# Half-logarithms of layer 2's row work on VectorE, a queue of its own for group 0, and a new placing of checks and waits in a four-layer graph kernel

## The chip, the cores and the metric

The kernel runs on one core of a Trainium2 chip. The core has a tensor engine for matrix products (TensorE; PE in the profile), a vector engine (VectorE, DVE), a scalar engine that evaluates functions from tables (ScalarE, ACT), a general engine (GpSimd, POOL), and a sequencer that issues most transfers here (SyncE, SP). [...] The metric is the device time of one execution in microseconds (us), given as the median of several executions.

## The reference

The input is a feature matrix x of 4096 rows by 64 features and an adjacency matrix adj of 4096 by 4096 zeros and ones. Four layers follow each other, each adding its result to its input and normalising every row:

```python
x = _layernorm(x + _L0_gnn_ref(x, adj, W, b))              # mean of neighbours, linear map, relu
x = _layernorm(x + _L1_gnn_ref(x, adj, r, w_att, b_att))   # hyperbolic attention
x = _layernorm(x + _L2_gnn_ref(x, adj, weight, bias))      # weights 0.5 ** (rank of the neighbour)
x = _layernorm(x + _L3_gnn_ref(x, adj, att_w, att_b))      # hyperbolic attention
```

Layers 1 and 3 weigh every edge with a sigmoid of a left number of the row and a right number of the neighbour. Both numbers come from `logmap0(x)`, whose factor is artanh(n)/n of the row's norm n; artanh is half the logarithm of (1+n)/(1-n). Layer 2 needs, for each row, the rank of each neighbour counted from the end, so that its weight is 2 to the power of minus that rank.

## The kernel before

The 4096 rows are cut into 4 groups of 1024 columns of the transposed adjacency matrix (`GROUPS` is 3, 2, 1, 0, in that order) and 32 blocks of 128 (also taken from the last to the first). Every layer reads the whole matrix again: `load(s, g)` (line 696) brings two blocks of one group, 1 MB, into one of 6 buffers called `edges`, through SyncE's queue; g runs from 15 down to 0. A buffer is used again six loads later, once its matmuls and its check are done.

`check` (line 834) is a test on VectorE that a loaded tile holds only zeros and ones; each tile is checked once in the whole kernel. Half of the checks are made in layer 0 (even g, line 1405) and half in layer 2 (odd g, `load_2`, line 1576).

Layer 0 and both attention layers run their passes one group at a time. Layer 2 runs a wide pass over groups 3 and 2 together (`wide_pass`, line 1517), then a narrow pass over group 1 and one over group 0 (`narrow_pass`, line 1544). Per block and half, TensorE counts neighbours into a `z` tile (`count`, line 1583), ScalarE takes an exponential of it (`weights_of`, line 1592), and TensorE multiplies the result with `halves`, the features times the layer's weight matrix.

What is done per row between the layers (here called row work) is written as Python generators. `later` puts a generator into one of two queues; `tick` takes each queue's first generator a step further, and a step says with `yield n` after how many ticks the next one may come. So ticks decide at which block of a pass the instructions of row work are written down. `need(tag)` ticks until the tagged work is written, however many ticks that takes, before the pass goes on. The order of TensorE and ScalarE is the written order (`FIXED`, line 589); the other engines are ordered by a planner from its own cost estimates. In the wide pass the first five blocks have no tick; from block 26 on there are two per block.

The generators that matter here:

- `move` (line 1096) turns an attention layer's sums for one group into new rows. For groups 3, 2 and 1 its row numbers are computed on GpSimd (with some steps on VectorE), for group 0 on VectorE. `pool_done` (line 661) gives the ticks that it leaves GpSimd. It ends with the rows of the next layer.
- `supports` (line 1245) follows the `move` of layer 1: a 16-bit copy of the rows on ScalarE and its remainder on GpSimd, 8 transposes, a copy on ScalarE, 16 small matmuls, a copy on ScalarE and a subtraction on VectorE give `halves` for the group. The wide pass needs group 1 before block 15 (tag `(2, 1)`) and group 0 before block 7 (tag `(2, 0)`).
- `attention` (line 1456) queues these: `supports` of groups 3, 2 and 1 in the second queue, `move` of each group in the first, and for the last group, group 0, both in the first queue, behind the `move` of group 1.
- `end_2` (line 1486), `norm_rows` (line 860) and `prepare` (line 880) turn the sums of layer 2 into the rows, factors and transposed features of layer 3. `prepare` also serves layer 1. Its second part, among casts and transposes, computes `t` (the norm) and `q1` (its square) on VectorE and takes two logarithms on ScalarE (lines 948 and 949); VectorE combines them (line 968) and forms left and right. In layer 3, groups 3 and 2 are prepared within the narrow passes, group 1 within the second one, group 0 at the start of the attention.

Between the exponentials of layer 2 and these logarithms ScalarE loads a table of functions, and another one to go back.

## Time and profile before

| what | value |
|---|---|
| runs | 1088.86, 1088.87, 1093.16 us; median 1088.87 |
| the profiled execution's own time | 1089.49 us |
| its span, first to last instruction | 1087.7 us |
| busy: TensorE, VectorE, ScalarE, GpSimd | 996.7, 913.4, 761.7, 265.0 us |
| layer 0, about 0 to 200 us | DMA busy 95% |
| attention of layer 1, about 200 to 511 us | TensorE busy 305.3 of 311 us |
| layer 2's wide pass, 511 to 617 us | TensorE busy 98.0 of 106 us |
| layer 2's narrow passes, 617 to 736 us | TensorE busy 104.9, ScalarE 98.1 of 119 us |
| attention of layer 3, 736 to 1050 us | TensorE busy 306.9 of 314 us |
| the end, 1050 to 1087.7 us | VectorE busy 22.5 of 37.7 us |

The span lies within the execution's own time; 1.8 us are around it. A line of the profile's timeline gives the start and the duration in us, the engine, the line of the kernel, the operation, the tiles written and read with their shapes, and in square brackets how long the engine had been idle before it and what ended that wait. A line with "x2" merges two instructions in a row. Layer 2 is the stage whose lines are named L1587 (counting), L1594 (exponential), L1599 and L1553 (sums). An `ACT_TABLE_LOAD` is ScalarE's change of its function table.

### The profile page before, as it was taken

The numbers are of one execution on the slowest core, as the hardware profiler recorded it, in microseconds if no ns is written. First come the engines' busy times: TensorE is split into PE (matmuls) and PEld (weight loads), VectorE is DVE, ScalarE is ACT, GpSimd is POOL, SyncE is SP. The second block draws the span as 40 slices with busy tenths as digits, with TensorE's granted clock in tenths as the row PEclk, the third lists the DMA queues.
The fourth block names the chain that finished last, engine by engine and source line by source line (L and its number), as shares of the span: only waits on it lengthen the run. The fifth ranks groups of instructions, "written<-read, shape, count | busy, mean of one in ns | idle before, by whom it ended". The sixth has DMA issues, their size and how long they took to land.

```text
span 1087.7 us, 13618 instructions
## 1 busy us (share of the span) xinstructions
PE 996.7 (92%) x4845; PEld 404.7 (37%) x4845; DVE 913.4 (84%) x1451; ACT 761.7 (70%) x888; POOL 265.0 (24%) x649
## 2 busy tenths in 40 slices
PE   5998998899999999999998988899899999999970
PEld 2455554233333333333333333443333333333320
DVE  6677978999999999999456494738999999999976
ACT  0003123879888989887675778889798988888850
POOL 0011211010154433514600010100001544344162
PEclk9998999899999999999999999999999999999995
DMA  9999999636576566655887988887366766666400
GB/s 344 399 418 378 359 427 390 223 130 242 194 252 213 199 230 214 230 200 185 309 302 295 359 289 291 283 280 256 131 224 210 254 210 218 240 217 226 148 1 23
DMA packets 38580, 271.62 MB, mean 250 GB/s; under 512 B 4710, under 2 KB 4710, under 8 KB 5734
## 3 DMA queue, kind: packets, MB, share of 16 engines
q1 hardware_dynamic: 37728, 270.03, 68.1%
q8 instruction: 40, 0.66, 0.2%
q10 hardware_dynamic: 774, 0.63, 0.2%
q14 instruction: 38, 0.31, 0.1%
HBM read 269.58 MB, written 1.05 MB: 249 GB/s over the span
## 4 chain that ended last, share of the span: by engine, by line
PE 62%; DVE 24%; ACT 6%; POOL 2%; DMA 2%; issue 2%; ACTq 0%; SPq 0%; POOLq 0%; DVEq 0%
PE acc L1035 17%; PE z L1587 9%; PE z L1057 8%; PE z L1063 7%; PE z L1060 7%; DVE t L1080 6%; DVE t L1078 6%; PE acc L1412 4%; DVE junk L836 3%; ACT sq L1594 2%; DMA edges<-in_adj_dram 2%; PE acc L1599 2%; ACT sq L1075 1%; PE z L1599 1%; PE aux L941 1%
## 5 line engine op out<-in xcount | busy, mean ns | idle before, releaser
L1078 DVE SCALAR_TENSOR_TENSOR t<-z,sig 128x1024 f32<-128x1024 f32 x256 | 309.9, 1220 | 13.9 <-ACT sq L1075 11.8
L1080 DVE SCALAR_TENSOR_TENSOR t<-sq,t 128x2048 f32<-128x2048 f32 x128 | 295.3, 2307 | 0.2
L1075 ACT ACTIVATE sq<-z 128x1024 f32<-128x1024 f32 x256 | 254.7, 1021 | 57.8 <-PE z L1063 25.6
L1072 ACT ACTIVATE sig<-left_b,right 128x1024 f32<-128x1024 f32 x256 | 287.2, 1149 | 3.9 <-DVE t L1078 2.9
L1035 PE MATMUL acc<-t,xe 128*64 128x512 f32 x1024 | 258.1, 610 | 10.9 <-DVE t L1080 10.7
L1057 PE MATMUL z<-edges,two_i 128*128 128x512 bf16 x512 | 202.5, 395 | 6.3 <-DVE t L1078 6.3
L1063 PE MATMUL z<-dst,src 74*128 74x512 f16 x512 | 196.4, 384 | 0.0
L1060 PE MATMUL z<-lo_hi,hi_lo 128*128 128x512 f16 x512 | 195.3, 381 | 0.0
L1594 ACT ACTIVATE sq<-z 128x512 bf16<-128x512 f32 (+1 forms) x192 | 136.7, 740 | 51.2 <-PE z L1587 48.0
L1035 PEld LDWEIGHTS acc<-t,xe 128*64 128x64 f32 x1024 | 64.0, 137 | 139.4 <-issue 105.9
L836 DVE SCALAR_TENSOR_TENSOR t<-edges 128x2048 bf16<-128x2048 f32 x32 | 73.0, 2287 | 35.2 <-DMA edges<-in_adj_dram 34.9
L1587 PE MATMUL z<-edges,pass_by 128*128 128x512 bf16 x248 | 89.1, 400 | 11.3 <-ACT sq L1594 10.9
L1412 PE MATMUL acc<-edges,first 128*128 128x512 bf16 x256 | 82.9, 406 | 14.3 <-DMA edges<-in_adj_dram 14.2
L1057 PEld LDWEIGHTS <-two_i 128*128 128x128 bf16 x512 | 50.4, 98 | 120.5 <-issue 74.5
L1587 PE MATMUL z<-edges,enter 128*128 128x512 bf16 x256 | 91.2, 399 | 0.0
L1412 PE MATMUL acc<-edges,third 128*65 128x512 bf16 x256 | 82.3, 404 | 0.0
L1063 PEld LDWEIGHTS <-src 74*128 74x128 f16 x512 | 49.5, 97 | 73.3 <-issue 11.8
L836 DVE SCALAR_TENSOR_TENSOR junk<-edges 128x2048 bf16<-128x2048 f32 x32 | 73.1, 2285 | 4.3 <-DMA edges<-in_adj_dram 4.0
L1060 PEld LDWEIGHTS <-hi_lo 128*128 128x128 f16 x512 | 50.4, 99 | 62.9 <-issue 17.4
L867 POOL TENSOR_TENSOR sq<-z 128x512 f32<-128x512 f32 x8 | 14.2, 1778 | 157.1 <-DVE z L866 134.0
L1131 POOL TENSOR_TENSOR w_att<-x,u 128x512 f32<-128x512 f32 x6 | 12.7, 2123 | 147.8 <-ACT u L1126 147.8
L1412 PEld LDWEIGHTS <-third 128*65 128x65 bf16 x256 | 29.3, 114 | 34.4 <-issue 5.4
(381 smaller groups left out, 981.5 us busy)
## 6 DMA issues: line engine op xcount, KB each, us to landing
edges<-in_adj_dram SPq DMA_DIRECT2D x256, 1024.0 KB, 4.9
x<-in_x_dram SPq DMA_DIRECT2D x4, 256.0 KB
out_dram<-x ACTq DMA_DIRECT2D x2, 256.0 KB
out_dram<-x SPq DMA_DIRECT2D x2, 256.0 KB
w_sb<-in_L_gnn_W_dram ACTq DMA_DIRECT2D x1, 32.0 KB, 4.8
w_twice<-in_L_gnn_weight_dram ACTq DMA_DIRECT2D x2, 16.0 KB, 7.8
given<-in_L_gnn_b_dram ACTq DMA_DIRECT2D x1, 0.2 KB
given<-in_L_gnn_bias_dram ACTq DMA_DIRECT2D x1, 0.2 KB
```

The source lines that it names most:

```text
L836: V.scalar_tensor_tensor(junk, a, 0.0, a, ALU.not_equal, ALU.not_equal, accum_out=odd[:, n : n + 1])
L1035: it = nc.tensor.matmul(acc[h * D : (h + 1) * D, :], xe[:, j, :], t[:, k, h * W : (h + 1) * W], start=j == BLOCKS[0], stop=j == BLOCKS[-1],)
L1057: nc.tensor.matmul(half, two_i, edge[:, at : at + W], start=True, stop=False)
L1060: nc.tensor.matmul(half, hi_lo[:, of], lo_hi[:, to], start=False, stop=False)
L1063: last = nc.tensor.matmul(half, src[:, of], dst[:, to], start=False, stop=True)
L1072: nc.scalar.activation(sig, left_b, AF.Sigmoid, bias=right[:, j : j + 1])
L1075: nc.scalar.activation(sq[:, k], zp, AF.Square, bias=ROOT + OFF, scale=-1.0 / UNIT)
L1078: V.scalar_tensor_tensor(t[:, k], zp, 0.0, sig, ALU.max, ALU.mult)
L1080: V.scalar_tensor_tensor(t, sq, HIGH**2, t, ALU.add, ALU.mult)
L1412: nc.tensor.matmul(accs[h][:m], lhs[:, j, :], edge[:, at : at + W], start=j == BLOCKS[0], stop=j == BLOCKS[-1],)
L1587: nc.tensor.matmul(z[:, h : h + W], lhs, rhs[:, h : h + W], start=j == BLOCKS[0], stop=True, skip_group_check=True,)
L1594: weighed[0] = nc.scalar.activation(w, z[:, :n], AF.Exp, bias=-(OFF_EDGE + CUT) * LN2, scale=-LN2)
```

## The change

It has five parts. `half_log_of_ratio` computes half the logarithm of (1+t)/(1-t) from (1+t) squared over (1-q): exponent and mantissa are taken apart by bit operations, and the mantissa's logarithm is a polynomial; all on VectorE. `prepare` calls it in layer 3 for groups 3, 2 and 1 in place of the two logarithms; group 0 and layer 1 keep them. A third queue takes `move` and `supports` of group 0 at the end of layer 1's attention. `checked_later` leaves the checks of g = 15 and 13 of groups 3 and 2 to layer 0 and those of g = 2 and 0 to layer 2. `pool_done` counts fewer ticks while layer 2 runs. So that the `move` of group 0 can run beside that of group 1, its `u` goes into another buffer, `z0`, and its sums are copied by VectorE.

```diff
--- before.py
+++ after.py
@@ -49,6 +49,8 @@
 MEAN_TOP = 1e-10
 
 LN2 = 0.6931471805599453
+ROOT2 = 2.0**0.5
+LOG = (0.3333341, 0.1998662, 0.14984541)
 OFF_EDGE = 255.0
 CUT = 27.0
 SUP = 512.0
@@ -588,7 +590,7 @@
 
             FIXED = {mybir.EngineType.PE, mybir.EngineType.Activation}
             ROW_ENGINES = FIXED | {mybir.EngineType.DVE}
-            queues, place, done, held = ([], []), [0, 0], set(), []
+            queues, place, done, held = ([], [], []), [0, 0], set(), []
 
 
 
@@ -627,7 +629,7 @@
                     mark(True)
 
             def later(steps, second=False, wait=0):
-                queues[second].append([steps, place[1] + wait])
+                queues[int(second)].append([steps, place[1] + wait])
 
             def in_turn(tag, *parts):
                 for part in parts:
@@ -640,7 +642,7 @@
 
             def need(tag):
                 while tag not in done:
-                    assert queues[0] or queues[1], tag
+                    assert any(queues), tag
                     tick(1)
 
             def soon():
@@ -660,6 +662,8 @@
 
             def pool_done(small, large=0):
 
+                if place[0] == 2:
+                    return 2 + int((small * 0.29 + large) / 1.45)
                 return 2 + int(small * 0.33 + large)
 
             spare, turn_of = [], [0]
@@ -698,6 +702,10 @@
                 nc.sync.dma_start(a, adj[s, :, 2 * g : 2 * g + 2, :])
 
                 return a, a.rearrange("p b i -> p (b i)").bitcast(BF16)[:, 1::2]
+
+            def checked_later(s, g):
+
+                return g in (0, 1, 2, 3, 5, 7, 9, 11) if s in GROUPS[:2] else g % 2 == 1
 
             def grp(name, bufs=None):
                 kw = {"bufs": bufs} if bufs else {}
@@ -856,6 +864,32 @@
                 V.tensor_scalar(sc, root, -((2.0 * UNIT) ** 0.5), None, ALU.mult)
                 V.tensor_scalar(short, root, least, None, ALU.mult)
                 return c, c2, sc, rsc, of_y, root, short, by_root, by_short
+
+            def half_log_of_ratio(t, q):
+
+                a, e, d = nums("log_a"), nums("log_e"), nums("log_d")
+                V.tensor_scalar(q, q, -1.0, 1.0, ALU.mult, ALU.add)
+                V.reciprocal(q, q)
+                V.tensor_scalar(a, t, 1.0, None, ALU.add)
+                V.tensor_mul(a, a, a)
+                V.tensor_mul(a, a, q)
+                V.tensor_scalar(
+                    e.bitcast(I32), a.bitcast(I32), 0x7F800000, None, ALU.bitwise_and
+                )
+                V.tensor_scalar(
+                    a.bitcast(I32), a.bitcast(I32), 0x007FFFFF, 0x3F800000,
+                    ALU.bitwise_and, ALU.bitwise_or,
+                )
+                V.tensor_scalar(e, e.bitcast(I32), 2.0**-23, -126.5, ALU.mult, ALU.add)
+                V.tensor_scalar(d, a, ROOT2, None, ALU.add)
+                V.reciprocal(d, d)
+                V.scalar_tensor_tensor(a, a, -ROOT2, d, ALU.add, ALU.mult)
+                V.tensor_mul(d, a, a)
+                V.tensor_scalar(q, d, LOG[2], None, ALU.mult)
+                V.scalar_tensor_tensor(q, q, LOG[1], d, ALU.add, ALU.mult)
+                V.scalar_tensor_tensor(q, q, LOG[0], d, ALU.add, ALU.mult)
+                V.scalar_tensor_tensor(q, q, 1.0, a, ALU.add, ALU.mult)
+                V.scalar_tensor_tensor(t, e, 0.5 * LN2, q, ALU.mult, ALU.add)
 
             def norm_rows(layer, s, v, x2_to):
 
@@ -927,6 +961,9 @@
                     V.tensor_mul(t, q1, rt)
                     V.tensor_scalar(t, t, TOP, None, ALU.min)
                     V.tensor_scalar(q1, q1, QTOP, None, ALU.min)
+                    by_log = layer == 3 and s != GROUPS[-1]
+                    if by_log:
+                        half_log_of_ratio(t, q1)
                     yield 2 * near()
                     for into, rows_of in (
                         (hi_lo, ys[:, :, : 2 * D]),
@@ -945,8 +982,9 @@
                         nc.scalar.copy(into[:, cols], turned[:n])
                         held.pop()
                         yield 1
-                    nc.scalar.activation(t, t, AF.Ln, bias=1.0)
-                    nc.scalar.activation(q1, q1, AF.Ln, bias=1.0, scale=-1.0)
+                    if not by_log:
+                        nc.scalar.activation(t, t, AF.Ln, bias=1.0)
+                        nc.scalar.activation(q1, q1, AF.Ln, bias=1.0, scale=-1.0)
                     yield from free()
                     p = take(F32, P, WB, 7)
                     for k in range(WB):
@@ -965,8 +1003,11 @@
                     )
                     V.tensor_mul(own, m, p[:, :, 6])
                     held.pop()
-                    V.scalar_tensor_tensor(f, q1, -0.5, t, ALU.mult, ALU.add)
-                    V.tensor_mul(f, f, rt)
+                    if by_log:
+                        V.tensor_mul(f, t, rt)
+                    else:
+                        V.scalar_tensor_tensor(f, q1, -0.5, t, ALU.mult, ALU.add)
+                        V.tensor_mul(f, f, rt)
                     V.scalar_tensor_tensor(f, f, SERIES0, q, ALU.add, ALU.add)
                     V.tensor_mul(f, f, m)
                     yield 1
@@ -1114,8 +1155,11 @@
                     all_u = ys.rearrange("p k f -> p (k f)").bitcast(F32)[:, : WB * (D + 1)]
                     all_u = all_u.rearrange("p (k f) -> p k f", f=D + 1)
                 else:
-                    all_u = row.tile([P, WB, D + 1], F32, name="u_1")
-                u, sum_1 = all_u[:, :, :D], all_u[:, :, D]
+                    all_u = None if last else row.tile([P, WB, D + 1], F32, name="u_1")
+                if all_u is None:
+                    u, sum_1 = grp("z0"), nums("sum_1")
+                else:
+                    u, sum_1 = all_u[:, :, :D], all_u[:, :, D]
                 for part in range(2):
                     yield from free()
                     t = take(F32, P, 2, 2, D + 1)
@@ -1123,9 +1167,18 @@
                         cols = slice((2 * part + i) * P, (2 * part + i + 1) * P)
                         nc.tensor.matmul(t[:, i], sums[:, cols], centre, start=True, stop=True)
                     yield near()
-                    nc.scalar.copy(
-                        all_u.rearrange("p (h k) f -> p k h f", h=2)[:, 2 * part : 2 * part + 2], t
-                    )
+                    of = slice(2 * part, 2 * part + 2)
+                    if all_u is None:
+                        nc.scalar.copy(
+                            u.rearrange("p (h k) f -> p k h f", h=2)[:, of], t[:, :, :, :D]
+                        )
+                        V.tensor_copy(
+                            sum_1.rearrange("p (h k) -> p k h", h=2)[:, of], t[:, :, :, D]
+                        )
+                    else:
+                        nc.scalar.copy(
+                            all_u.rearrange("p (h k) f -> p k h f", h=2)[:, of], t
+                        )
                     held.pop()
                     yield near()
                 E.tensor_mul(w, xg, u)
@@ -1402,7 +1455,7 @@
                             a, edge = load(s, g)
                             if s == GROUPS[0] and 2 * g % WB == WB - 2 and g > WB // 2:
                                 parts_of(2 * g // WB - 1)
-                            if g % 2 == 0:
+                            if not checked_later(s, g):
                                 check(s, g, a, own.tile([P, 2, WW], BF16, name="junk"))
                             for k in (1, 0):
                                 j = 2 * g + k
@@ -1468,9 +1521,10 @@
                             in_turn((layer + 1, s + 1), there((layer, s + 1, "moved")), behind(s + 1)),
                             True, 9,
                         )
-                    later(move_s)
+                    apart = 2 if n + 1 == NW and layer == 1 else 0
+                    later(move_s, apart)
                     if n + 1 == NW:
-                        later(in_turn((layer + 1, s), behind(s)))
+                        later(in_turn((layer + 1, s), behind(s)), apart)
                 anchored[0] = False
 
 
@@ -1575,7 +1629,7 @@
 
             def load_2(s, g):
                 a, edge = load(s, g)
-                if g % 2 == 1:
+                if checked_later(s, g):
                     junk = sb.tile([P, 2, WW], F32, name="t", bufs=3).bitcast(BF16)
                     check(s, g, a, junk[:, 0, :].rearrange("p (b i) -> p b i", b=2))
                 return edge
```

## The prediction

> **What bounds the kernel now.** I first read the busy times by stage, since the change sits in layer 2 and, through the checks, in layer 0. Columns: stretch and length, busy us (and instructions) of PE, PEld, DVE, ACT, POOL, PE clock, DMA share, GB/s.
>
> ```profile
> 0.00:200.00 200.00, 176.09 (x970) 97.14 (x972) 155.15 (x449) 42.27 (x64) 22.42 (x41) 0.95 0.95 384
> 511.00:617.00 106.00, 97.96 (x570) 37.06 (x567) 57.39 (x124) 68.94 (x76) 19.43 (x53) 0.98 0.78 293
> 617.00:736.00 119.00, 104.90 (x546) 48.48 (x542) 73.13 (x225) 98.12 (x165) 11.35 (x24) 0.96 0.83 296
> ```
>
> Layer 0 is bound by transfers, the wide pass by TensorE, the narrow passes by the ring between TensorE and ScalarE; VectorE has room in both passes. Next the timelines of TensorE and ScalarE in layer 2, for where they stop.
>
> ```profile
> 559.79 0.71 PE L1124 MATMUL aux<-centre,sums 128*128 128x130 f32 x4
> 560.34 0.61 PE L1124 MATMUL z<-centre,sums 128*128 128x130 f32 x4
> 561.80 0.62 PE L1256 MATMUL aux<-ident,x_hl 128*128 128x128 f16 x8 [0.85 <-POOL x_hl L1251]
> 563.52 0.64 PE L1266 MATMUL z<-w_hl,x_t 128*128 128x64 f16 x16 [1.10 <-ACT x_t L1259]
> ...
> 589.89 0.62 PE L1256 MATMUL aux<-ident,x_hl 128*128 128x128 f16 x8 [2.67 <-POOL x_hl L1251]
> 591.61 0.64 PE L1266 MATMUL z<-w_hl,x_t 128*128 128x64 f16 x16 [1.10 <-ACT x_t L1259]
> ```
>
> These are the two places where `supports` was forced out by `need`, all steps at once with no block between them. Then the logarithms of group 3 in a narrow pass (group 2's at 701.44 look the same):
>
> ```profile
> 659.32 1.08 ACT L1594 ACTIVATE sq<-z 128x512 bf16<-128x512 f32 x2
> 660.42 1.28 ACT L948 ACT_TABLE_LOAD   x1
> 661.72 0.21 ACT L948 ACTIVATE tt<-tt 128x8 f32<-128x8 f32 x1
> 661.83 0.19 ACT L949 ACTIVATE q<-q 128x8 f32<-128x8 f32 x1
> 662.04 1.28 ACT L1594 ACT_TABLE_LOAD   x1
> 663.34 1.08 ACT L1594 ACTIVATE sq<-z 128x512 bf16<-128x512 f32 x2
> ```
>
> Last, VectorE where attention 1 ends, and the start of layer 0:
>
> ```profile
> 509.99 1.22 DVE L1078 SCALAR_TENSOR_TENSOR t<-z,sig 128x1024 f32<-128x1024 f32 x1
> 511.12 2.28 DVE L836 SCALAR_TENSOR_TENSOR t<-edges 128x2048 bf16<-128x2048 f32 x1
> ...
> 513.33 2.29 DVE L1080 SCALAR_TENSOR_TENSOR t<-sq,t 128x2048 f32<-128x2048 f32 x1
> ```
>
> ```profile
> 22.08 0.80 PE L820 MATMUL aux<-one_row,att_row 1*128 1x1 f32 x4 [3.65 <-DVE given_b L1330]
> ```
>
> A check stands ahead of the attention's last product. At 22 us TensorE waits for a VectorE copy that stands behind two checks (17.19 and 19.54).
>
> [...] both switches and both logarithms lie within 660.40 to 663.34, 2.94 us[...]. [...] after 2.52 us of idle before 663.98 the matmuls start 0.425 us apart instead of 0.225, until 667.3. [...] here 128x8 takes 0.17, and 0.20 from start to start in a dependent chain. [...]
>
> **The change part by part**, against the profiled execution (1089.49; span 1087.7 and 1.8 around it).
>
> *Logarithms.* A pair of exponentials normally comes every 1.36 us (622.80 to 624.16). From 659.32 to 667.63 there are three pairs, 8.31 us against 4.08: 4.23 lost, of which the table changes are about 2.6 and the slow clock after them the rest. Group 2's, 700.33 to 708.65, lose 4.24. The 8 small matmuls of line 953 stay (0.28 from start to start, part hidden), so I take 8.4 for both. Group 1's stand at the end, ahead of the copy of the sums at 736.24; the last sum ends at 735.3, so 0.9 goes. The load for the sigmoids at 737.31 stays, and group 0's logarithms too. Sum 9.3.
> In their place come 17 instructions, less one at line 968: 16 x 0.20 = 3.2 us per group, 9.6 on VectorE. The bit operations and their integers aren't in the trace; nearest is the integer 128x8 TENSOR_SCALAR, 0.17, and I bound one at 0.15 to 0.25, so 2.4 to 4.0 per group. They can start once `q1` is there (650.6, 669.8, 710.3) and are wanted at 660.1, 701.1 and 736; VectorE sits idle for 7.13 us ahead of 660.07, 3.02 ahead of 672.89 and 16.65 ahead of 736.37. So nothing is added; without that cover a check or an `ys` subtraction behind it is late by up to 4.0 per group, 12 in all.
>
> *Queues and waits.* I counted the yields. Before, at layer 2's first tick `move` of group 1 has its reciprocal to write; it is done at tick 23, in `need`'s first flush of 8 ticks, and group 0's `move` only begins there; its `supports` takes a second flush of 7. After, group 1's waits fall from 5, 8 and 9 ticks to 4, 6 and 7: `supports` starts at tick 18 (block 18) and a flush of 2 ticks, with one copy and one subtraction, is left. Group 0 begins at tick 1: tanh at tick 11 (block 21), `supports` at 25 (block 15), done at 31 (block 12), well ahead of block 7. The chain of `supports` then has blocks of 2.89 us between its steps.
> A block's first matmuls come every 2.894 us (519.28 to 556.90, 13 blocks). The first stop lasts 556.90 to 564.00, 4.21 too long; its matmuls remain, its waits, 0.85 + 1.10 = 1.95, go. The second loses 4.95, of which waits of 2.67 + 1.10 = 3.77 go, and the slow block after it (592.09 to 596.54) gives 1.56. Sum 7.3.
> Are the operands there? Group 1: GpSimd needed 19.6 us after the reciprocal (522.17 to 541.81); without checks ahead, the reciprocal can run at about 513.5, rows are there at 533, and are wanted at 553. GpSimd's steps now run beside VectorE's for group 0; at twice the time it still holds. Group 0: VectorE took 8.0 us before tanh, 2.0 of them for `supports`; from 534.6 that gives 540.6, wanted at 543.4. After tanh 14.7 less two checks (4.6), so 10.1: 553.5, plus up to four checks that land there (9.2): 562.7, wanted at 561.8. ScalarE waits in order, so a late tanh or cast holds the exponentials behind it, and TensorE behind them. I set 0.8 aside (bounds 0 and 7.3): gain 6.5. ScalarE has 0.95 us spare per block; the moved copies (1.0 at most) fit. VectorE's new sum copies (nearest: 0.18 for 128x4 from PSUM) fall into its idle time around 531; the planner could put them behind a check, which would hold `free` up by 2.3, inside that bound.
>
> *Checks.* As many as before. With none at g = 15 and 13 in layer 2, the last product of attention 1 can follow at 511.2 instead of 513.33, and all behind it: 2.2 (bounds 0 and 2.3). At the wide pass's end 8 checks instead of 4 fall in the last four g: 18.3 us in 23.2. They are made as tiles land, some 6 us before their use, so the buffers, hence SyncE's loads, aren't held; uncovered, one costs 2.3.
> In layer 0 each of groups 3 and 2 gets two checks more in its first four tiles. Group 3: the copy at 21.75 stands behind the checks; one more puts it, TensorE, and then the load that waited until 29.17 for a buffer 2.3 later. Nine tiles of 2.5 us and the rows of x had kept transfers busy until about there, so it is paid in full unless planned behind the copy; g = 15's check can use the 5.6 us that VectorE waited before 16.95. Group 2: row work (57 to 85) meets one check more; its check at 79.26 already held a load (81.62) and half of the DMA's time in 80 to 82.5. With 2.4 us of short gaps in that row work I take 0.7. Neither end's dropped checks (45.83, 50.77, 91.48, 93.82) gated a transfer. Loss 3.0, bounds -1.0 (the plan closes a gap) and 9.2 (all four paid).
>
> **Sum:** 9.3 + 6.5 + 2.2 - 3.0 = 15.0. The profiled execution would take 1074.5, its span 1072.7; the median of the runs lies 0.6 lower, so 1088.9 - 15.0 = 1073.9.
>
> **The rivals.** *VectorE becomes what the wide pass waits for* (0.18). For it: group 0's rows are wanted 0.9 us before my late bound, and the planner can put checks first. Against it: VectorE is busy for only 18.2 of the 40.3 us from 517.7 to 558. Only logarithms and the first product gain: 9.3 + 2.2 - 3.0 = 8.5, 1080.4. *Layer 0 hides its checks* (0.13): g = 13's is planned behind the copy and a gap closes: loss 0 to -1.0, so 18 to 19, or 22 if the dip at 125 to 135 shrinks too: 1067 to 1071. *No change* (0.07): the DMA-bound stage pays all four checks, 9.2, and rival one holds: 9.3 + 2.2 - 9.2 = 2.3, 1086.6. *Slower* (0.05): on VectorE, ahead of group 0's row work, stands a check whose tile has yet to land. The trace shows such waits (6.93 before 542.18), 9.2 with the check itself. ScalarE's tanh or cast then stops both passes' engines, buffers come free late, and the next check waits as well. From two such waits on, 18.4, the 18.0 gained in layer 2 is gone, and with layer 0's 3.0 it is slower: 1092. Against it: before, such waits only occur where nothing else was to do.
>
> **How the numbers follow.** The forecast has 0.57, from 1071 to 1077. Under 1067 I leave 0.06, over 1082 0.13; so 1067 to 1082. Measurement of this kernel can tell 0.5%, 5.4 us: faster below 1083.4, slower above 1094.3; of the slower rival's 0.05 I put 0.04 above. Faster 0.88, same 0.08, slower 0.04.
>
> **What would show it.** No table load within layer 2's narrow passes, and no matmuls 0.42 apart behind them; TensorE's waits at lines 1256 and 1266 gone, the wide pass near 97 us; the 16 new instructions in idle time; the attention's last product right behind line 1078; in layer 0 the copy of line 1330 near 24 and the attention some 3 us later. I am wrong if ScalarE waits for VectorE at lines 1162 or 1250, if SyncE's loads wait for checks in layer 2, or if layer 0 loses more than 5.

## The result, and the profile after

The changed kernel takes 1074.59 us in the median of six runs (1072.09 to 1078.91), where the kernel before took 1091.38 in its six (1088.86 to 1093.78). The ratio is 0.9851, with an interval from 0.9826 to 0.9876. The profiled execution took 1073.46, its span 1071.7, against 1089.49 and 1087.7.

All times by stage below come from profiles and are cut at instructions that both kernels have. A runs from the start to the load of the exponential's table at the end of attention 1. B runs from there to ScalarE's copy of the wide pass's sums, C to the copy at the end of group 1's narrow pass, D to that at the end of group 0's, and E to the end of the span.

| stage | before | after | difference |
|---|---|---|---|
| A: layer 0, attention 1 | 510.18 | 512.19 | +2.01 |
| B: end of attention 1, wide pass | 107.16 | 97.98 | -9.18 |
| C: narrow pass of group 1 | 59.47 | 55.84 | -3.63 |
| D: narrow pass of group 0 | 59.43 | 53.65 | -5.78 |
| E: attention 3, end | 351.46 | 352.04 | +0.58 |
| span | 1087.7 | 1071.7 | -16.0 |

Not all of these are equally exact. D is 53.6 to 53.7 in nine of the kernels with the half-logarithms. C repeats within 0.1 where two kernels have the same steps and TensorE's clock is slow for as long (a longer slow stretch makes it about 1 us longer; the last section says when). B is 97.96 to 97.98 in four of the six kernels that share its queues, waits and checks of groups 3 and 2, and 98.8 to 98.9 in the other two. A and E move by several us from one profile to the next: A lies between 506.9 and 518.2 in all that follow, so its +2.01 alone tells little.

The busy times by stage of the kernel after, with the columns of the prediction, answer to its first view:

```profile
0.00:200.00 200.00, 170.50 (x964) 95.05 (x965) 152.95 (x447) 41.61 (x63) 24.44 (x41) 0.97 0.95 383
512.00:610.00 98.00, 97.16 (x574) 36.95 (x576) 59.80 (x126) 69.52 (x76) 16.70 (x53) 1.00 0.86 317
610.00:720.00 110.00, 100.22 (x540) 47.30 (x538) 79.78 (x277) 91.62 (x156) 14.87 (x24) 0.98 0.88 316
```

In the wide pass TensorE is now idle for 0.84 us of 98, where it was for 8.0 of 106. In the narrow passes it still sits idle for 9.8 of 110; that remainder is what the later experiments are about. TensorE's timeline in the wide pass, at the transposes and small matmuls of `supports` (line 1309 was 1256, line 1319 was 1266):

```profile
557.94 0.62 PE L1309 MATMUL aux<-ident,x_hl 128*128 128x128 f16 x8
...
561.54 0.64 PE L1319 MATMUL z<-w_hl,x_t 128*128 128x64 f16 x16 [0.19 <-ACT x_t L1312]
...
566.01 0.62 PE L1309 MATMUL aux<-ident,x_hl 128*128 128x128 f16 x8
```

Of the four waits that the prediction showed, 5.72 us together, 0.19 is left. Next is ScalarE's timeline where group 3's logarithms stood; no table is loaded, and the exponentials keep their step of 1.36 us (line 1648 was 1594):

```profile
654.12 1.20 ACT L1648 ACTIVATE sq<-z 128x512 bf16<-128x512 f32 x2 [0.28 <-PE z L1641]
655.48 1.21 ACT L1648 ACTIVATE sq<-z 128x512 bf16<-128x512 f32 x2 [0.15 <-PE z L1641]
656.84 1.20 ACT L1648 ACTIVATE sq<-z 128x512 bf16<-128x512 f32 x2 [0.15 <-PE z L1641]
```

VectorE at the end of attention 1 (line 1119 was 1078, line 1121 was 1080). Only a small reciprocal stands ahead of the last product, where a check of 2.28 us stood:

```profile
512.01 1.22 DVE L1119 SCALAR_TENSOR_TENSOR t<-z,sig 128x1024 f32<-128x1024 f32 x1
513.14 0.19 DVE L1233 RECIPROCAL den<-den 128x8 f32<-128x8 f32 x1
513.26 2.29 DVE L1121 SCALAR_TENSOR_TENSOR t<-sq,t 128x2048 f32<-128x2048 f32 x1
```

And TensorE's wait near 22 us in layer 0, which was 3.65 and is now longer and later:

```profile
23.58 1.01 PE L828 MATMUL aux<-one_row,att_row 1*128 1x1 f32 x4 [4.41 <-DVE given_b L1383]
```

One thing was in no line of the prediction. In the first narrow pass TensorE has a new stop. Two views of the kernel after, VectorE's timeline and TensorE's, both cut to the lines that matter:

```profile
614.11 0.41 DVE L1560 SCALAR_TENSOR_TENSOR z<-aux,given_b 128x256 f32<-128x256 f32 x1
...
615.16 2.29 DVE L844 SCALAR_TENSOR_TENSOR t<-edges 128x2048 bf16<-128x2048 f32 x1
...
622.15 2.28 DVE L844 SCALAR_TENSOR_TENSOR t<-edges 128x2048 bf16<-128x2048 f32 x1
...
626.38 0.42 DVE L1560 SCALAR_TENSOR_TENSOR z<-z,given_b 128x256 f32<-128x256 f32 x1
```

```profile
623.01 0.39 PE L1641 MATMUL z<-edges,enter 128*128 128x512 bf16 x1
626.85 0.59 PE L1607 MATMUL z<-sq,halves 128*128 128x512 bf16 x1 [3.44 <-DVE z L1560]
627.23 0.63 PE L1641 MATMUL z<-edges,pass_by 128*128 128x512 bf16 x1
```

The two lines 1560 read the sums of groups 3 and 2. Between them lies part of group 3's row work, and in it two checks (line 844). TensorE waits until the second read has freed the `z` tile, and then runs its matmuls 0.43 us apart in place of 0.225 until 630.16. In the kernel before that wait was 1.35.

### The profile page after: what moved, and what is told of

It reads as the page before. It is cut to its first block, busy times and chain, and to the rows that moved or that the text cites. A ratio compares the mean times of both kernels' runs of the same rounds, so it can differ in the third digit from the quotient of the medians.

```text
span 1071.7 us, 13656 instructions
## 1 busy us (share of the span) xinstructions
PE 985.7 (92%) x4845; PEld 401.4 (37%) x4845; DVE 919.6 (86%) x1501; ACT 754.4 (70%) x877; POOL 272.3 (25%) x649
## 4 chain that ended last, share of the span: by engine, by line
PE 61%; DVE 25%; ACT 6%; DMA 3%; POOL 2%; issue 2%; ACTq 0%; SPq 0%; POOLq 0%; DVEq 0%
PE acc L1076 17%; PE z L1641 9%; PE z L1098 8%; PE z L1104 7%; PE z L1101 7%; DVE t L1119 6%; DVE t L1121 6%; PE acc L1465 4%; DVE junk L844 3%; DMA edges<-in_adj_dram 2%; ACT sq L1648 2%; PE acc L1653 2%; ACT sq L1116 1%; PE z L1653 1%; ACT sig L1113 1%
## 5 line engine op out<-in xcount | busy, mean ns | idle before, releaser
L1641 PE MATMUL z<-edges,enter 128*128 128x512 bf16 x256 | 88.8, 389 | 0.0
L1465 PEld LDWEIGHTS <-first 128*128 128x128 bf16 x256 | 24.3, 98 | 45.1 <-issue 16.2
```

The lines of the kernel that those rows point to most:

```text
L1465: nc.tensor.matmul(accs[h][:m], lhs[:, j, :], edge[:, at : at + W], start=j == BLOCKS[0], stop=j == BLOCKS[-1],)
L1641: nc.tensor.matmul(z[:, h : h + W], lhs, rhs[:, h : h + W], start=j == BLOCKS[0], stop=True, skip_group_check=True,)
```

## The experiments

**The logarithms alone, and all but them.** The first of these two kernels has only the half-logarithms, with the queues, waits, checks and buffer of before; the second is the changed kernel without them.

```diff
# e1_log_alone, against the changed kernel
-                return g in (0, 1, 2, 3, 5, 7, 9, 11) if s in GROUPS[:2] else g % 2 == 1
+                return g % 2 == 1
-                if place[0] == 2:
-                    return 2 + int((small * 0.29 + large) / 1.45)
-                    apart = 2 if n + 1 == NW and layer == 1 else 0
+                    apart = 0
-                    all_u = None if last else row.tile([P, WB, D + 1], F32, name="u_1")
+                    all_u = row.tile([P, WB, D + 1], F32, name="u_1")
# e2_no_log, against the changed kernel
-                    by_log = layer == 3 and s != GROUPS[-1]
+                    by_log = False
```

> The kernel before with the half-logarithm on VectorE as its only edit. If the gain of the narrow passes is that of the table loads and of the slow matmuls behind them, this alone is 9.3 us faster than before (ratio 0.9915), all of it between the copies of the wide pass's sums and the start of the sigmoids, and the wide pass stays at 106 us. If the narrow passes gain for another reason (the wide pass leaves them earlier rows), the time stays within 2 us of before.

> The changed kernel with its two logarithms back on ScalarE. If the parts add up, it is 16.0 - 9.4 = 6.6 us faster than before (ratio 0.994) and its narrow passes again lose about 4.2 us at each of two places and 1.5 to 2 at their end. If the queue and the waits only pay together with the logarithms, it is within 2 us of before.

The logarithms alone: 1084.02 us, ratio 0.9928 (0.9904 to 0.9953). All but them: 1084.54, ratio 0.9942 (0.9919 to 0.9965). By the medians the gains are 7.5, where 9.3 was expected, and 6.9, where 6.6 was; both expected ratios lie inside the intervals. Together they are 14.4 of the 16.8 of the whole, which the intervals allow.

The profiles are sharper. With the logarithms back on ScalarE C is 60.04 and D 59.40, with them on VectorE 55.84 and 53.65: 4.20 and 5.75, together 9.95. Of D's 5.75, 1.55 is the end of the pass: the copy of the sums followed the start of the last pair of exponentials after 2.61 us before (733.63 to 736.24) and follows after 1.06 now (718.60 to 719.66). ScalarE's next table load starts 2.0 us sooner behind that pair (3.68 before, 1.66 after), but one copy of the sums, some 0.6, now stands behind the load. Alone, however, moving the logarithms took 5.72 from C, not 4.2. The remaining 1.5 isn't theirs, as the next two views show. Both kernels have the same stop of TensorE, 2.42 us, 20 us ahead of the place of the logarithms. In the kernel before TensorE came out of it at half clock:

```profile
640.40 0.59 PE L1587 MATMUL z<-edges,pass_by 128*128 128x512 bf16 x1 [2.42 <-ACT sq L1594]
640.78 0.63 PE L1587 MATMUL z<-edges,enter 128*128 128x512 bf16 x1
641.21 0.63 PE L1553 MATMUL acc<-sq,halves 128*128 128x512 bf16 x1
```

With the logarithms alone on VectorE, it came out at full clock:

```profile
645.50 0.39 PE L1639 MATMUL z<-edges,pass_by 128*128 128x512 bf16 x1 [2.42 <-ACT sq L1646]
645.73 0.39 PE L1639 MATMUL z<-edges,enter 128*128 128x512 bf16 x1
645.95 0.38 PE L1605 MATMUL acc<-sq,halves 128*128 128x512 bf16 x1
```

So a logarithm's place is worth 4.2, as predicted, and 1.5 is the price of a slow stretch of TensorE's clock, which the same stop brought in one kernel and not in the other.

**The computation twice.** The half-logarithm is first computed on copies, and that first result is not used; so VectorE's price is more than doubled, and nothing else in the program changes.

```diff
# e4_log_twice, in half_log_of_ratio
+                t_2, q_2 = nums("spare_t"), nums("spare_q")
+                V.tensor_copy(t_2, t)
+                V.tensor_copy(q_2, q)
+                half_log_spare(t_2, q_2)
```

> The changed kernel with each half-logarithm computed twice on VectorE, the first time on copies whose result nobody reads: 19 more instructions of 0.20 us, 3.8 us per group, ahead of the real ones. If VectorE's cost lies in its idle time, layer 2 takes as long as in the changed kernel to 1 us. If VectorE is on the path, the narrow passes take up to 11 us longer.

1075.73 us in one run; C 55.90 and D 53.64, as in the changed kernel to 0.1. B, in which no half-logarithm stands, is 0.8 longer, with a wait of 0.49 for VectorE's part of `halves` (565.78) that the changed kernel doesn't have. In the changed kernel one half-logarithm took from 645.42 to 648.42, 3.0 us. VectorE has room for two of them in each place.

**Where there is no room.** The same formula for group 0 too, whose row work lies inside attentions 1 and 3.

```diff
-                    by_log = layer == 3 and s != GROUPS[-1]
+                    by_log = layer == 3 or s == GROUPS[-1]
```

> Half-logarithms by VectorE for group 0 too, whose row work lies inside attentions 1 and 3, where VectorE has no idle time to lend. That takes two table loads and two short activations from ScalarE (1.28 + 1.28 + 0.4 = 2.96 us) and gives 17 instructions to VectorE, twice. My theory (VectorE sets the pace of the attentions, so here the new instructions have no cover): between 17 x 0.08 = 1.4 us, if each comes between two independent ones, and 17 x 0.2 = 3.4 us, if they come one behind the other, in each attention; so 3 to 7 us slower than the changed kernel, 1078 to 1081, with both narrow passes as before (55.8 and 53.7). Rival (a table load is on the path wherever it stands, and ScalarE sets the pace): 2 x 2.96 = 5.9 us faster, near 1068.7.

1080.67 us, ratio 0.9892 (0.987 to 0.9914), against 0.9851 (0.9826 to 0.9876) for the changed kernel: 6.1 us more by the medians, though the intervals just meet, where the rival wanted 5.9 less. The expectation's two steps are those of the kernel before: there independent 128x8 instructions of VectorE start 0.07 apart (632.52 and 632.59), dependent ones 0.20 (628.44 and 628.64). Taking table loads from ScalarE isn't a gain in itself; it was one where ScalarE and TensorE alternate and VectorE waits. In attention 1 VectorE was busy for 301.1 of 311 us before. From the first sigmoid's table to the end of attention 1 the profile takes 324.1 and E 355.3, where the other twelve profiles have 321.2 to 323.3 and 351.2 to 354.3. So both are the longest of all, though two table loads are gone from each; how much was lost there isn't settled. B, C and D are 2.5 longer too. In B 0.9 is a wait for VectorE's part of `halves` (571.48); in C, with the same stops as in the changed kernel, the half clock lasts twice as long (632.92 to 639.74).

**The checks as before.**

```diff
-                return g in (0, 1, 2, 3, 5, 7, 9, 11) if s in GROUPS[:2] else g % 2 == 1
+                return g % 2 == 1
```

> The changed kernel with the checks where they were (odd g in layer 2 for all groups). Theory: layer 0 gets back the 2.0 us that it lost, attention 1 ends with a check in front of its last product again (1.9 to 2.2 later), so the sum moves by less than 1 us. Rival: the early checks in layer 2 hold group 0's row work, so that tanh or the cast of its rows is late and the wide pass loses 3 to 7 us more.

1077.11 us, ratio 0.988 (0.9851 to 0.9909), 2.5 more than the changed kernel, with intervals that overlap. The start of B, from the table load to the copy of attention 1's sums, takes 7.49 again (7.48 before, 5.59 after): the check ahead of the last product costs 1.9. The rest of B takes 93.85 instead of 92.39, with a wait of TensorE of 1.49 for VectorE's part of `halves` (562.61), less than the 3 to 7 of the rival. So the moved checks bring 3.4 in layer 2. C is 56.90 instead of 55.84, but that isn't theirs: its stops are the same (3.45 and 1.16), and after the first one TensorE's clock is halved until 630.44, for 5.5 us, where the changed kernel has 3.2. The sum of the runs leaves about -0.9 for the rest, layer 0 above all, with an uncertainty of some 4 us, so nothing that this run can tell.

**Eight early checks in layer 0.** To make layer 0's price larger than the scatter:

```diff
-                return g in (0, 1, 2, 3, 5, 7, 9, 11) if s in GROUPS[:2] else g % 2 == 1
+                return g < 8 if s in GROUPS[:2] else g % 2 == 1
```

> Groups 3 and 2 check their blocks 15 to 8 in layer 0 and 7 to 0 in layer 2: of the first eight blocks that layer 0 loads of each group all eight are checked at once, where the changed kernel checks five and the kernel before four. Theory of the prediction (each check that comes early in layer 0 holds VectorE for 2.3 us ahead of a row step that is wanted): up to the end of attention 1 the kernel needs 3 to 9 us more than the changed one, near 1080. Rival (layer 0 waits for its transfers, and VectorE's checks lie in idle time): the same time, within 2 us of 1074.6, as long as the wide pass and the narrow passes stay at 92.4, 55.8 and 53.7.

The expectation miscounts: of these eight blocks the changed kernel checks six, not five, so the two groups have four early checks more, as many as the change itself added. 1081.00 us, ratio 0.9905 (0.9885 to 0.9925), and the changed kernel's interval ends below it: 6.4 more. In the profile 0.9 of it is in B, where TensorE now waits 0.91 for GpSimd's part of the 16-bit copy (572.20). C is 1.1 longer with the same stops, again by a half clock of twice the length (631.84 to 638.66); D doesn't move. That leaves 4.4 to 5.5 for A and E, about 1.1 to 1.4 for each early check. Layer 0 itself shows it: SyncE issues its last load at 180.2, where the twelve other profiles lie between 171.1 and 177.9. That further early checks cost nothing is refuted; 3.0 for the change's own four fits, but neither run settles it to a microsecond.

**Own queue and shorter waits, one by one.**

```diff
# e5_one_queue
-                    apart = 2 if n + 1 == NW and layer == 1 else 0
+                    apart = 0
# e6_old_waits
-                if place[0] == 2:
-                    return 2 + int((small * 0.29 + large) / 1.45)
# e7_neither: both edits
```

> The changed kernel with group 0's move and supports back in the first queue, behind group 1's; waits, checks and logarithms as changed. By the counted yields group 1's supports then start at tick 18 and group 0's move only there, so that its supports come out in a flush of 7 ticks ahead of block 7. From the table load of the exponentials to the copy of the wide pass's sums the changed kernel takes 98.0 us; here it should take about 104, the second stop of the kernel before (3.8 of waits and 1.6 of slow matmuls) and part of the first. If the queue is without effect because VectorE or GpSimd set the time, it stays at 98.

> The changed kernel with the longer waits for GpSimd. Group 1's supports then start at tick 23, in a flush of 7 ticks ahead of block 15 in which group 0's supports begin too. The same stretch should take about 100 to 101 us instead of 98.0: the first stop returns (1.95 of waits), the second doesn't.

> The changed kernel without its own queue and without the shorter waits, that is with the changed checks and logarithms alone. Both stops return in full: 98.0 + 7.3 = 105.3 us for the same stretch. If this is much less than 105, the stops of the kernel before came from its early checks, not from its queue.

One run each: 1083.6, 1084.43 and 1085.33 us, with B at 104.89, 104.91 and 106.12. Without the start of B, the wide pass takes 99.31 with one queue, 99.32 with the old waits, 100.53 with neither and 92.39 with both. So each edit alone brings 1.2, and both together 8.1. I had expected the own queue alone to bring most. TensorE's timeline with the own queue and the old waits says why:

```profile
567.98 0.62 PE L1307 MATMUL aux<-ident,x_hl 128*128 128x128 f16 x8 [2.94 <-POOL x_hl L1302]
570.27 1.04 PE L1317 MATMUL z<-w_hl,x_t 128*128 128x64 f16 x16 [1.67 <-ACT x_t L1310]
```

The busy times of this kernel, for the stretch around it, in the columns of the first view:

```profile
565.00:575.00 10.00, 5.17 (x55) 3.75 (x55) 2.62 (x3) 4.86 (x7) 3.30 (x2) 0.72 0.24 73
```

Group 1 is still late, and group 0, which is early, doesn't help: the 16-bit copies of both groups come within 3.6 us (565.1 and 568.7), and their `supports` are written down in one heap. TensorE works for 5.17 of 10 us and its clock falls to 0.72. With the short waits and one queue it is the other way round: group 1 has one wait left (1.55), and group 0 starts behind it and stops the pass at 592.75 and 594.48 (2.81 and 1.10). The wide pass has two due points, and each edit meets only one of them.

**The checks in the first narrow pass.** The stop of 3.44 was tested by moving checks of group 1 only: in the first kernel block 14 is checked in layer 2 in place of 13, in the second also block 10 in place of 11. The number of checks stays the same.

```diff
# e8_check_14 (in e10_checks_14_10: (1, 3, 5, 7, 9, 10, 14, 15))
-                return g in (0, 1, 2, 3, 5, 7, 9, 11) if s in GROUPS[:2] else g % 2 == 1
+                return g in (0, 1, 2, 3, 5, 7, 9, 11) if s in GROUPS[:2] else g in (1, 3, 5, 7, 9, 11, 14, 15) if s == 1 else g % 2 == 1
```

> The changed kernel with one check of group 1 exchanged: layer 2 checks g = 14 instead of 13, layer 0 the other one. In the changed kernel the check at 615.16 lies between the row work of group 3, and TensorE waits 3.44 us at 626.85 for VectorE's read of group 2's sums behind it. g = 14 lands one tile earlier, in VectorE's idle time from 605.9 to 613.8. Theory: the first narrow pass takes 53.7 us, as with the logarithms alone, instead of 55.8, and the whole 2 us less than the changed kernel. Rival: the check at 622.15 (g = 11) holds the read anyway, and nothing changes by more than 0.5.

> Group 1 checks its blocks 14 and 10 in layer 2 in place of 13 and 11 (13 and 11 in layer 0 in place of 14 and 10), so that in the written order no check stands between the first read of the sums of group 3 and that of group 2. My theory (the new stop of TensorE in the first narrow pass is the checks that stand there): TensorE waits at most 1.3 us for the spare of line 1560 in place of 3.44, the pass of group 1 takes 53.0 to 53.8 us in place of 55.84, and the kernel 1072 to 1073. Rival (the stop moves to the next wait of the pass, that of the table of squares or of the matmuls of the rows): the pass stays over 55, no gain. A third: layer 0 loses what the pass gains, since its checks now stand elsewhere: pass near 53.5, time unchanged.

With one check moved: 1074.13 us, ratio 0.985 (0.9821 to 0.9879), C 54.57: 1.3 less, where I expected 2.1 of C, and nothing that the runs can tell. With both: 1070.42 us, ratio 0.9825 (0.98 to 0.9849), C 51.62 and D 54.14. This is the fastest of the kernels here by its median, 4.2 below the changed one, although the intervals of the two overlap; in the profiles C is 4.2 shorter and D 0.5 longer. VectorE's timeline of it, reads of the sums and checks, shows no check between the two reads:

```profile
611.97 0.41 DVE L1560 SCALAR_TENSOR_TENSOR z<-aux,given_b 128x256 f32<-128x256 f32 x1
...
621.56 0.42 DVE L1560 SCALAR_TENSOR_TENSOR z<-z,given_b 128x256 f32<-128x256 f32 x1
...
623.09 2.29 DVE L844 SCALAR_TENSOR_TENSOR t<-edges 128x2048 bf16<-128x2048 f32 x1
```

TensorE's timeline of it has this wait in place of 3.44:

```profile
622.04 0.38 PE L1607 MATMUL z<-sq,halves 128*128 128x512 bf16 x1 [0.78 <-DVE z L1560]
```

The terms of C now add up over the kernels in which the half clock lasts for one stretch of 3.4 us or doesn't come. "First stop" is the wait for line 1560 (1506 before), "second" that for the exponentials behind the casts of `ys`. "Slow clock" says whether the matmuls ran 0.43 apart after one of them worth 1.5, about half of the slow time; "logarithms" are 4.2. The last column adds each kernel's differences from the bottom row to that row's 51.62.

| kernel | checks between the reads | first stop | second stop | slow clock | logarithms on ScalarE | C | sum |
|---|---|---|---|---|---|---|---|
| before | 1 | 1.35 | 2.42 | yes | yes | 59.47 | 59.2 |
| logarithms alone | 1 | 1.36 | 2.42 | no | no | 53.75 | 53.5 |
| one queue | 1 | 1.33 | 2.68 | no | no | 53.77 | 53.7 |
| after | 2 | 3.44 | 1.16 | yes | no | 55.84 | 55.8 |
| all but the logarithms | 2 | 3.45 | 1.15 | yes | yes | 60.04 | 60.0 |
| one check moved | 1 | 2.07 | 1.37 | yes | no | 54.57 | 54.6 |
| both checks moved | 0 | 0.78 | 1.15 | no | no | 51.62 | |

The kernels with the old waits and with neither fit too: 55.84 with stops of 3.41 and 1.21 and a slow clock, 53.75 with 1.34, 2.69 and none. In the three kernels with a half clock of twice the length (the checks as before, eight early checks, the half-logarithms for group 0 too), C is 56.90 to 57.14.

So C's -3.63 in the changed kernel is -4.2 for the logarithms and +0.6 for the second check that had come into the row work. The planner puts it there because of the own queue: with one queue (the same checks and waits) one check runs ahead of the first read and only one lies between the two. The table also says why one moved check disappointed: the slow clock stayed. Of the 4.2 that both moved checks brought, 2.7 is the stop and 1.5 the slow clock.

## Why the prediction was right, and where it wasn't

The predicted 1073.9 is within 0.7 of the median, and the forecast's case is the one that came. That it is so close is in part luck. The kernel before took 1091.38 in these runs and not the 1088.9 that I subtracted from, so the gain was 16.8 by the medians (16.0 by the spans) and not 15.0; and a stop that I hadn't counted was made up for by terms that I had set too low.

- *Logarithms, 9.3.* Right in mechanism and size: 4.20 in C and 4.20 + 1.55 in D, 9.95. The end of the pass was sized at 0.9 and measured 1.55. That VectorE's instructions lie in idle time is shown by the run with two computations; 3.2 us were estimated for one, 3.0 measured, and an integer 128x8 takes 0.17 as its nearest row did.
- *Queues and waits, 7.3 less 0.8.* The wide pass gave 7.29 (99.68 to 92.39). The 0.8 that I set aside for late operands wasn't needed: ScalarE waited for neither tanh nor cast. What such a wait does stands in the kernel before: ScalarE was idle for 1.15 us ahead of the cast of line 897 at 638.20, the exponential behind it, whose last matmul had ended at 637.11, began at 639.76, and TensorE stopped for 2.42. GpSimd's doubled time was an estimate; in the kernel before a 128x8 product of line 759 took it 2.17 during the check of 530.64 and 0.20 at 535.94, in the changed kernel (line 767) 0.20 each of the four times from 520.31 to 526.03. The new checks have a part in it (93.85 with the old ones), and I counted none. Each of the two edits alone brings only 1.2 of the 8.1 that they bring together.
- *The last product, 2.2.* 1.9 measured, by the start of B: 7.48 to 5.59, and back to 7.49 with the old checks.
- *Layer 0, -3.0.* The sign is shown by the run with eight early checks; the size isn't settled. The step that I named can't be told from scatter: the copy came at 23.24 and the load behind it at 30.23, 1.5 and 1.1 later than before and not 2.3; but with the same early checks as before the copy stood at 18.95 (the checks as before) and 21.96 (the logarithms alone). The two checks added ahead of it (7.57 and 12.66) lie in time that VectorE mostly had: of the 5.62 us that it was idle ahead of its next step, 2.54 are left. The issue of layer 0's last load says more: 171.1 to 176.6 in the three kernels with the early checks of before, 174.2 to 177.9 in the nine with those of the change, 2.2 later by the means.
- *VectorE has room in the narrow passes.* This is the step that failed, though not for the half-logarithms that I asked it about. Idle time summed over a pass is no cover for a check that falls into the chain between two reads of the sums. The stop of 1.35 was in the profile before and had no line in my sum; of the checks near the wide pass's end I only asked whether they hold buffers. It cost 0.6 against the kernel before, and 4.2 against what the same number of checks allows. Of the signs of being wrong that I named, one came in small: in the narrow passes SyncE's loads waited twice for a check, 1.2 us together, but TensorE waited for no landing there.
- *The rivals.* VectorE as the wide pass's wait is out, since the waits at 1309 and 1319 are 0.19 together; but the room is small, as three kernels wait 0.5 to 1.5 there for its part of `halves`. A layer 0 that hides its checks is refuted for four further ones by the run with eight; for the change's own four the later last load speaks against it, within the scatter. The other two, no change and slower, did not come.

The own sum of the parts, 9.95 + 7.29 + 1.9, less 0.6 for the new stop and 2.6 for A and E together, is 15.9 (16.0 by the spans); the forecast had 15.0. The last 2.6 stays open between layer 0 and scatter.

## What to carry to other kernels

Price a table change on ScalarE by the step it breaks and by which engine has idle time there: 17 small VectorE instructions in place of two loads saved 4.2 to 5.75 us in each narrow pass, and the same exchange gained nothing, and by the medians lost, where VectorE was busy for 301 of 311 us. Where an optional step shares an engine with a chain that others wait for, look at the written order inside that chain, not at the engine's idle sum: here the place of two checks was worth 4.2 us of one pass. And when two row groups have two due points in a pass, expect little from bringing one group forward alone: 1.2 of 8.1 here.

## What the runs showed of the hardware that was not expected

The prediction has a stop of TensorE of 2.52 us with half clock behind it; not every such stop has that. One of 2.42 us brought 3.3 us of half clock in the kernel before (640.40 to 643.67) and none, at the same place, with the logarithms alone; one of 2.68 brought none with one queue. One of 2.07 us did, with one check moved, and there the slow stretch only began 1.1 us after the work had resumed, as TensorE's timeline of that kernel shows:

```profile
626.78 0.39 PE L1641 MATMUL z<-edges,pass_by 128*128 128x512 bf16 x1
627.00 0.49 PE L1641 MATMUL z<-edges,enter 128*128 128x512 bf16 x1
627.29 0.63 PE L1607 MATMUL z<-sq,halves 128*128 128x512 bf16 x1
```

It ended near 630.6, 3.4 us later. Stops of 1.37 and less brought none in these passes.

The traces show what goes with it. They record the granted clock, and in each of the 13 every change of it lies on one grid of 3.41 us, which stands at another place from trace to trace. A stretch from one point of the grid to the next is called a window here. Cut into windows, with the columns of the first view, the kernel before has 2.16 of its 2.42 us in one window. TensorE is busy there for 1.26 us, and the next window runs at half clock (the 0.50 in the third column from the end):

```profile
636.73:640.14 3.41, 1.26 (x6) 0.47 (x5) 3.41 (x8) 2.26 (x5) 3.15 (x7) 1.00 0.98 387
640.14:643.56 3.42, 3.16 (x8) 1.15 (x8) 3.42 (x11) 1.89 (x4) 0.95 (x3) 0.50 0.43 180
```

With the logarithms alone the same stop is shared by two windows, and neither is followed by half clock:

```profile
641.35:644.76 3.41, 1.74 (x8) 0.67 (x7) 3.41 (x10) 2.25 (x5) 2.83 (x6) 1.00 0.93 327
644.76:648.18 3.42, 2.68 (x12) 1.15 (x12) 3.42 (x7) 2.97 (x7) 1.41 (x3) 1.00 0.63 256
648.18:651.59 3.41, 3.41 (x23) 1.70 (x22) 3.37 (x30) 2.66 (x5) 0.00 (x0) 1.00 0.79 250
```

With one check moved, the window that holds the stop of 2.07 ends at 627.14:

```profile
623.73:627.14 3.41, 1.34 (x7) 0.58 (x6) 3.41 (x10) 1.04 (x3) 0.00 (x0) 1.00 1.01 365
627.14:630.56 3.42, 3.42 (x10) 1.16 (x8) 3.42 (x10) 1.95 (x4) 2.64 (x4) 0.50 0.18 77
```

And with the checks as before, the first window at half clock still holds a part of the stop, and a second one follows. This is the longer slow stretch that made C 1 us longer in three kernels:

```profile
623.62:627.03 3.41, 2.12 (x6) 0.73 (x6) 3.38 (x13) 0.59 (x1) 0.00 (x0) 0.50 0.50 209
627.03:630.44 3.41, 3.41 (x10) 1.18 (x9) 3.41 (x10) 1.42 (x4) 2.24 (x5) 0.50 0.00 0
```

The 13 traces together have 869 such windows at full clock between 505 and 740 us. In 18 of them TensorE was busy, by the profile, for less than 45% of the window, 1.5 us, and half clock followed each of these. Of the 851 others half clock followed two, both near the end of group 0's pass with the logarithms on ScalarE. Of the 25 windows at half clock, the five with up to 2.55 us of work were followed by another one, the 20 with 2.82 and more by full clock. So half clock followed windows that weren't idle throughout, with up to 1.5 us of work in them. What sets the grid, the traces don't show. No run moved a stop against the windows on purpose; that they stood elsewhere in each execution did it by chance.

For the reader of a profile: a stop of two to three microseconds has a second price of about 1.5 us that may or may not appear, one of 3.4 can have it twice, and a difference of that size between two profiles needs a look at the granted clock before it is put down to an edit.
